# A four-byte-per-row store of zeros as the first transfer of a DMA-bound kernel

## The chip, the cores and the metric

The kernel runs on one core of a Trainium2 chip. The metric is the device time of one execution in microseconds (us). The median of three runs of the kernel before is 324.08 us, from 323.89 to 324.3.

## The reference

There are 128 samples; each is a matrix `x[b]` of 128 channels by 1024 time steps, in float32. Each sample names one of 8 subjects, and each subject has a 128 x 128 weight matrix. The sample's matrix is multiplied by its subject's weights over the channels, and the product is added to the sample:

```python
def _L0_cond_ref(x, subjects, weights):
    B, C, D, T, N_SUBJECTS = (128, 128, 128, 1024, 8)
    w = weights[subjects]
    out = jnp.einsum('bct,bcd->bdt', x, w)
    return out
x = x + _L0_cond_ref(x, itok_B_0_7, L0_cond_weights)
```

A sample is 512 KB. All of `x` is 67.1 MB read from HBM, and the output is 67.1 MB written to it; the weights of all subjects are 512 KB.

## The kernel before

The samples are taken in 32 tiles of four (`G = 2` samples in each of `H = 2` halves). The on-chip memory holds a ring of `SLOTS = 12` tiles of 2 MB, `x_all`; a tile is loaded into a slot, the products are added to it in place, and the result is stored from the same slot.

Each engine has its own list of work, written out by hand, and semaphores order the lists among one another:

- ScalarE issues all loads (the function `load`, through `transfer`, whose line in the profile is L57), one sample each, on its own transfer queue, q10. From tile 12 on it first waits until the slot's stores have landed.
- SyncE issues the load of the subject numbers (`given`, L179), the load of all weights (`w_all`, L180) and then all stores (the function `store`, L57 too), on its queue q1. A store waits for VectorE's additions (`s_added`). The first and the last tile are stored in halves, all others whole. The very last sample has a store of its own (L238), issued after ScalarE has waited for the other stores.
- VectorE clears `zeros` (L182), turns the subject numbers into indices (L192 to L198), copies the chosen weights of each sample into one of four small tiles (`place`, L152), and adds the products, which stand in PSUM, to the samples in the slot (`add`, L173).
- TensorE first multiplies zeros three times (`IDLE`, L185) and then, for each half tile, waits for the weights (`s_go`) and for the samples (`s_ready`) and does four products of 512 columns (`multiply`, L157 and L161).
- GpSimd turns the completion of loads into the semaphore `s_ready`.

Both queues run on the same 16 DMA engines. A transfer adds 16 to its semaphore when all of it has landed (`DMA = 16`). Constants such as a column of zeros (`const-float32-0.0`, 128 rows of one element) are filled by GpSimd before the lists begin.

Of the kernel before, what the change touches and what calls it, by code (L numbers as in the profile page):

```python
# [25 lines left out]
F32 = mybir.dt.float32  # L26
# [13 lines left out]
DMA = 16  # L40
# [30 lines left out]
def kernel(  # L71
# [7 lines left out]
    nc = tc.nc  # L79
    B, C, T = x.shape  # L80
# [21 lines left out]
        ctx.enter_context(nc.psum_tensor(f"ps{i}", [D, G, T], F32)).ap() for i in range(P_SLOTS)  # L102
    ]

    s_given = tc.alloc_semaphore("s_given")
    s_wall = tc.alloc_semaphore("s_wall")
    s_index = tc.alloc_semaphore("s_index")
# [11 lines left out]
    def emptied(i):  # L119
        turns = i // SLOTS  # L120
        return DMA * (H * G + 1) * turns - (DMA * G if i >= SLOTS and i % SLOTS == 0 else 0)

    def load(engine, i, q):
        transfer(
            nc,
            engine,
            xs[i % SLOTS][:, q, :],
            x[i * H * G + q].rearrange("(a r) t -> a (r t)", r=ROWS),
        ).then_inc(s_head if i * H * G + q < G else s_slot[i % SLOTS], DMA)

    def store(i, q0, q1):
        b = i * H * G
        transfer(
            nc,
            nc.sync,
            out[b + q0 : b + q1].rearrange("g d t -> d g t"),
            xs[i % SLOTS][:, q0:q1, :].rearrange("d (o g) t -> d o (g t)", g=min(G, q1 - q0)),
        ).then_inc(s_first if i == 0 and q1 == G else s_slot[i % SLOTS], DMA)

    def subjects_of(i):  # L140
        _, subject = nc.values_load_multi_w_load_instructions(
            index[0:1, i] if isinstance(i, slice) else index[0:1, bass.ds(i * (H * G), H * G)],
            engines=[mybir.EngineType.DVE],
            min_val=0,
            max_val=S - 1,
            skip_runtime_bounds_check_because="the index is clamped on the chip above",
        )
        return subject

    def place(h, subject):  # L150
        for q in range(h * G, (h + 1) * G):
            copy = nc.vector.tensor_copy(ws[q], w_all[:, bass.ds(subject[q], 1), :])  # L152
        copy.then_inc(s_go, 1)

    def multiply(slot, h):
        nc.tensor.wait_ge(s_go, 1).then_inc(s_go, -1)
        nc.tensor.wait_ge(s_ready, 1).then_inc(s_ready, -1)  # L157
        for q in range(h * G, (h + 1) * G):
            for t in range(0, T, N):
                at = slot * (H * G * T) + (q * T + t)  # L160
                mm = nc.tensor.matmul(  # L161
                    ps[h][:, q % G, t : t + N],
                    ws[q][:, 0, :],
                    x_all[:, bass.ds(at, N)],
                    start=True,
                    stop=True,
                )
        mm.then_inc(s_product, 1)

    def add(slot, h):  # L170
        mine = x_all[:, bass.ds(slot * (H * G * T) + h * G * T, G * T)]
        nc.vector.wait_ge(s_product, 1).then_inc(s_product, -1)  # L172
        nc.vector.tensor_tensor(  # L173
            mine, ps[h].rearrange("d g t -> d (g t)"), mine, ALU.add
        ).then_inc(s_added, 1)

    with tc.tile_critical():  # L177

        nc.sync.dma_start(given, subjects.rearrange("(o b) -> o b", o=1)).then_inc(s_given, DMA)  # L179
        nc.sync.dma_start(w_all, weights.rearrange("s c d -> c s d")).then_inc(s_wall, DMA)  # L180

        nc.vector.memset(zeros, 0.0).then_inc(s_zeros, 1)  # L182
        nc.tensor.wait_ge(s_zeros, 1)
        for _ in range(IDLE):
            nc.tensor.matmul(  # L185
                ps[P_SLOTS - 1][:, G - 1, :N], zeros[:, :D], zeros, start=True, stop=True
            )

        nc.vector.memset(index[:, B:], 0).then_inc(s_index, 1)  # L192
        nc.vector.wait_ge(s_given, DMA)
        nc.vector.tensor_scalar(near, given, -S, S - 1, ALU.max, ALU.min).then_inc(s_index, 1)  # L194
        nc.vector.wait_ge(s_index, 2)
        nc.vector.tensor_scalar(wrap, near, 0, S, ALU.is_lt, ALU.mult).then_inc(s_index, 1)  # L196
        nc.vector.wait_ge(s_index, 3)
        nc.vector.tensor_tensor(index[:, :B], near, wrap, ALU.add).then_inc(s_index, 1)  # L198
        for i in range(NT):
            if i == SLOTS:  # L200
                nc.scalar.wait_ge(s_first, DMA)
            if i >= SLOTS:
                nc.scalar.wait_ge(s_slot[i % SLOTS], emptied(i))
            for q in range(H * G):
                load(nc.scalar, i, q)

        for i in range(NT):
            if i == 0:
                nc.gpsimd.wait_ge(s_head, DMA * G).then_inc(s_ready, 1)
                nc.gpsimd.wait_ge(s_slot[0], DMA * G).then_inc(s_ready, 1)  # L210
            else:
                nc.gpsimd.wait_ge(s_slot[i % SLOTS], emptied(i) + DMA * H * G).then_inc(s_ready, H)

        for i in range(NT):
            for h in range(H):
                if i in (0, NT - 1) or h == H - 1:
                    nc.sync.wait_ge(s_added, i * H + h + 1)
                    store(i, h * G if i in (0, NT - 1) else 0, (h + 1) * G - (i * H + h == NT * H - 1))


        nc.vector.wait_ge(s_index, 4)
        nc.vector.wait_ge(s_wall, DMA)
        subject = subjects_of(slice(0, H * G))
        for h in range(H):
            place(h, subject)
        with nc.vector.Fori(0, NT) as turn:  # L226
            subject = subjects_of(turn + 1)
            for h in range(H):
                add(turn % SLOTS, h)
                place(h, subject)  # L230
        with nc.tensor.Fori(0, NT) as turn:
            for h in range(H):
                multiply(turn % SLOTS, h)
# [39 lines left out]
```

## Time and profile before

| What | Value |
|---|---|
| Median of three runs | 324.08 us |
| The profiled execution's own time | 324.3 us |
| Its span, first to last instruction | 322.5 us |
| Moved over HBM | 67.63 MB read, 67.11 MB written |
| Mean rate over the span | 418 GB/s |
| Mean granted TensorE clock | 0.92 |
| VectorE's additions (L173) | 64, 2291 ns each |
| Loads of a sample (512 KB) | 128, median 31.6 us from issue to landing |
| Stores of a tile (2 MB) | 30, median 47.1 us from issue to landing |
| Load of the weights (512 KB) | 5.2 us from issue to landing |

The profile is of one execution, and all its times count from the first instruction. Of each group of instructions it tells the busy time, the mean of one, and what ended the idle time before it. A view by windows gives, for chosen stretches of time, each engine's busy time with the number of its instructions, then the granted TensorE clock, the mean busy share of the 16 DMA engines, and the rate in GB/s. Bytes and busy time of a transfer packet are put down to the moment at which it starts, so that a share can exceed 1 in a short stretch. The trace also keeps a record of every single packet, with its start, length, size and queue.

### The profile page before, as it was taken

The page shows a single profiled execution, that of the slowest core. Times are in us where ns is not written, and L with a number is a line of the kernel's source. Part 1 is how long each engine was busy: PE and PEld are TensorE (multiplying, and loading weights), DVE is VectorE, ACT ScalarE, POOL GpSimd, SP SyncE. Part 2 cuts the span into 40 slices and gives each one's busy share as a digit, 9 for nine tenths or more (in the row PEclk, how much of TensorE's full clock was granted, in tenths as well). Part 3 has the DMA queues.
Part 4 walks back from the last instruction along what each step waited for, and adds up shares of the span by engine and source line. Part 5 has one row for each costly group of instructions (what it writes and reads, how often), then busy time and mean ns, then how long its engine had stood idle before and what let it go on. Part 6 is the DMA issues. An engine that isn't in the chain of part 4 may idle for free. (4 is left out here: it accounts for less than half of the span.)

```text
span 322.5 us, 2381 instructions
## 1 busy us (share of the span) xinstructions
PE 237.1 (74%) x518; PEld 98.1 (30%) x518; DVE 165.7 (51%) x202; POOL 0.2 (0%) x4
## 2 busy tenths in 40 slices
PE   5999998888888888888888888888885995500000
PEld 2434433333333333333333333333331432100000
DVE  2267776666566566666656655666666263600000
POOL 0000000000000000000000000000000000000000
PEclk9799999999999999999999999999999798955555
DMA  7999999999999999999999999999999999999996
GB/s 276 427 391 421 427 428 421 427 429 435 417 427 433 421 425 423 431 427 427 423 424 431 433 419 424 430 426 426 433 426 418 428 425 423 428 429 425 426 425 288
DMA packets 16067, 134.76 MB, mean 418 GB/s; under 512 B 2625, under 2 KB 3650, under 8 KB 3906
## 3 DMA queue, kind: packets, MB, share of 16 engines
q1 hardware_dynamic: 9922, 67.64, 50.0%
q10 hardware_dynamic: 6144, 67.12, 49.5%
q14 instruction: 1, 0.01, 0.0%
HBM read 67.63 MB, written 67.11 MB: 418 GB/s over the span
## 5 line engine op out<-in xcount | busy, mean ns | idle before, releaser
L161 PE MATMUL ps<-x_all,w 128*128 x512 | 232.7, 609 | 39.7 <-PEq L157 39.7
L173 DVE TENSOR_TENSOR x_all<-ps,x_all 128x2048 f32 x64 | 146.6, 2291 | 109.4 <-DVEq L172 109.4
L161 PEld LDWEIGHTS ps<-x_all,w 128*128 128x128 f32 x512 | 96.4, 193 | 176.0 <-issue 175.8
L152 DVE COPY w<-w_all 128x128 f32 x132 | 23.1, 218 | 4.2 <-DMA w_all<-in_L_cond_weights_dram 4.2
L185 PE MATMUL ps<-zeros 128*128 128x512 f32 x6 | 4.4, 890 | 1.7 <-DVE zeros L182 1.7
L185 PEld LDWEIGHTS ps<-zeros 128*128 128x128 f32 x6 | 1.7, 305 | 3.5 <-issue 1.9
L182 DVE MEMSET zeros<- 128x512 f32 x1 | 0.5, 485 | 1.0 <-SPq L177 1.0
L194 DVE TENSOR_SCALAR near<-given 1x128 int32<-1x128 int32 x1 | 0.2, 216 | 0.8 <-DMA given<-in_itok_B_dram 0.8
L198 DVE CUSTOM_DVE_ANT_0 index<-near,wrap 1x256 uint16<-1x256 uint16 x1 | 0.3, 278 | 0.0
L196 DVE TENSOR_SCALAR wrap<-near 1x128 int32<-1x128 int32 x1 | 0.2, 215 | 0.0
L260 POOL MEMSET const-bfloat16-1.0<- 128x1 bf16 x1 | 0.1, 101 | 0.0
L260 POOL MEMSET const-uint8-127<- 128x1 uint8 x1 | 0.1, 101 | 0.0
L260 POOL MEMSET const-float32-0.0<- 128x1 f32 x1 | 0.1, 98 | 0.2 <-issue 0.2
L260 POOL MEMSET const-float32-1.0<- 128x1 f32 x1 | 0.1, 98 | 0.0
L260 DVE BASE_LOAD x1 | 0.0, 15 | 0.1
L192 DVE MEMSET index<- 1x4 int32 x1 | 0.1, 62 | 0.0
## 6 DMA issues: line engine op xcount, KB each, us to landing
x_all<-in_x_dram ACTq DMA_DIRECT2D x128, 512.0 KB, 31.6
out_dram<-x_all SPq DMA_DIRECT2D x30, 2048.0 KB, 47.1
out_dram<-x_all SPq DMA_DIRECT2D x3, 1024.0 KB, 14.4
out_dram<-x_all SPq DMA_DIRECT2D x2, 512.0 KB, 20.6
w_all<-in_L_cond_weights_dram SPq DMA_DIRECT2D x1, 512.0 KB, 5.2
given<-in_itok_B_dram SPq DMA_DIRECT2D x1, 0.5 KB
```

Source lines behind the costliest of these rows:

```text
L152: copy = nc.vector.tensor_copy(ws[q], w_all[:, bass.ds(subject[q], 1), :])
L161: mm = nc.tensor.matmul(ps[h][:, q % G, t : t + N], ws[q][:, 0, :], x_all[:, bass.ds(at, N)], start=True, stop=True,)
L173: nc.vector.tensor_tensor(mine, ps[h].rearrange("d g t -> d (g t)"), mine, ALU.add).then_inc(s_added, 1)
L182: nc.vector.memset(zeros, 0.0).then_inc(s_zeros, 1)
L185: nc.tensor.matmul(ps[P_SLOTS - 1][:, G - 1, :N], zeros[:, :D], zeros, start=True, stop=True)
L192: nc.vector.memset(index[:, B:], 0).then_inc(s_index, 1)
L194: nc.vector.tensor_scalar(near, given, -S, S - 1, ALU.max, ALU.min).then_inc(s_index, 1)
L196: nc.vector.tensor_scalar(wrap, near, 0, S, ALU.is_lt, ALU.mult).then_inc(s_index, 1)
L198: nc.vector.tensor_tensor(index[:, :B], near, wrap, ALU.add).then_inc(s_index, 1)
L260: nc = _bacc.Bacc("TRN2", target_bir_lowering=False, num_devices=1)
```

## The change

SyncE's first transfer is now a store of zeros to the output of sample 0: the first element of each of its 128 rows, so 128 pieces of 4 bytes, 4096 bytes apart. Its source is the constant column of zeros. Behind it on the same queue come the loads of subjects and weights. Before the first real store, which writes the same addresses again, SyncE waits until the small store has landed (`s_opened`).

```diff
+    s_opened = tc.alloc_semaphore("s_opened")
     s_given = tc.alloc_semaphore("s_given")
...
     with tc.tile_critical():
 
+
+        nc.sync.dma_start(
+            out[0, :, :1],
+            nc.const_aps.tensor(0.0, (C, 1), F32),
+            allow_slow_non_contiguous=True,
+        ).then_inc(s_opened, DMA)
         nc.sync.dma_start(given, subjects.rearrange("(o b) -> o b", o=1)).then_inc(s_given, DMA)
         nc.sync.dma_start(w_all, weights.rearrange("s c d -> c s d")).then_inc(s_wall, DMA)
...
+        nc.sync.wait_ge(s_opened, DMA)
         for i in range(NT):
             for h in range(H):
                 if i in (0, NT - 1) or h == H - 1:
```

## The prediction

> **What bounds the kernel now.** I read the page first, its busy shares, slices and queues.
>
> ```profile
> span 322.5 us, 2381 instructions
> PE 237.1 (74%) x518; PEld 98.1 (30%) x518; DVE 165.7 (51%) x202; POOL 0.2 (0%) x4
> DMA  7999999999999999999999999999999999999996
> GB/s 276 427 391 421 427 428 421 427 429 435 417 427 433 421 425 423 431 427 427 423 424 431 433 419 424 430 426 426 433 426 418 428 425 423 428 429 425 426 425 288
> q1 hardware_dynamic: 9922, 67.64, 50.0%
> q10 hardware_dynamic: 6144, 67.12, 49.5%
> ```
>
> TensorE works 74% of the span and VectorE 51%. The two transfer queues (q1 is SyncE's, q10 ScalarE's) together hold the 16 DMA engines for 99.5% of it. The slices have one visible dip after the start: the third, 391 against about 426 GB/s. The windows by time locate it (the columns are busy times, the TensorE clock, the DMA share and GB/s).
>
> ```profile
> 2.00:8.00 6.00, 4.05 (x6) 1.36 (x5) 1.30 (x7) 0.00 (x0) 1.00 1.02 369
> 8.00:18.00 10.00, 9.44 (x18) 4.09 (x19) 3.15 (x5) 0.00 (x0) 0.83 1.00 424
> 18.00:24.00 6.00, 6.00 (x15) 2.46 (x13) 4.58 (x6) 0.00 (x0) 1.00 0.99 373
> 24.00:60.00 36.00, 34.01 (x78) 14.39 (x78) 24.48 (x28) 0.00 (x0) 1.00 1.01 426
> 319.00:322.50 3.50, 0.00 (x0) 0.00 (x0) 0.00 (x0) 0.00 (x0) 0.50 0.28 115
> ```
>
> From 18 to 24 us the engines are as busy as ever (0.99) and deliver 373 in place of 426 GB/s: 6 us x (1 - 373/426) = 0.75 us of transfer lost. Before it loads alone reach 424; after it loads and stores together reach 426. So neither stream is slow in itself; the change from one to the other costs something. The timeline and the waits say what starts then.
>
> ```profile
> 0.94 0.35 SPq L179 DMA_DIRECT2D given<-in_itok_B_dram  x1
> 1.35 0.42 SPq L180 DMA_DIRECT2D w_all<-in_L_cond_weights_dram  x1
> 16.40 0.65 SPq L57 DMA_DIRECT2D out_dram<-x_all  x1
> DVE w L152 <- DMA w_all<-in_L_cond_weights_dram: 4.2, 1, 4.2
> SPq L269 <- DMA out_dram<-x_all: 19.2, 1, 19.2
> ```
>
> The first store is issued at 16.40, so the dip is the first writing to HBM. The DMA view of 18 to 20.7 us sharpens it:
>
> ```profile
> q10 hardware_dynamic: 87, 0.95, 103.6%
> ```
>
> That is the only data queue listed: 4.3 us after the issue no store packet has begun. In the records of single packets the first one begins at 20.78. The weights, also issued behind queued loads, took from 1.35 to 3.80, or 2.45 us; the first store took 1.9 us more. Meanwhile load packets stretch: 16 KB takes 613 ns on average from 8 to 18 us, 979 ns from 19.5 to 20.7, with 1102 the longest, on all engines at once, and 615 from 24 to 60. Store packets take 310 ns from the first on. I read this as a price paid once, when the first writes to the output go out.
>
> **The change, part by part.** The sums are made against the profiled execution: span 322.5, and 1.8 us around it, 324.3 us. The median of the runs is 324.08, 0.22 less; I carry that to the end.
>
> The added transfer's issue on SyncE: the two neighbours took 0.35 and 0.42 us, so I take 0.4. It moves the issue of the subjects (`given`) to about 1.35 and of the weights to 1.75. VectorE waits for the weights until 7.41, then come the copies at L152, the first product at 8.56 and the first store at 16.40; all of this slips by 0.4 us, or by up to 1.9 more if the writes keep their opening delay and the weights wait behind them. The cover is ScalarE's queue: loads are issued from 0.90 until about 60 us without needing more than their slots, and 12 slots of 2 MB are 25.2 MB, 59 us at 424 GB/s. At the other end the last VectorE work ends at 281.3 us while stores run to 321, 40 us of stores in hand. So a first store 0.4 to 2.3 us late costs nothing; without that cover it would cost its whole length.
>
> The wait on `s_opened` stands on SyncE in front of the first store's wait; behind it are all stores. The transfer should land by about 6 us, and SyncE waits for VectorE until 16.40 in any case: nothing. The price comes only if the landing needs 15 us.
>
> The added packets: 128 of 4 bytes, 8 for each of 16 engines if they are spread as other 128-row transfers are. No row shows a 4-byte write to HBM. Nearest rows, from single packets: the 4-byte completion marks take 9 ns, the weights' 512-byte packets 27, the longest of these 155. That makes 0.07, 0.22 or 1.24 us per engine, all of it on the path, as the engines have no idle time. A price below nothing is excluded, since the bytes of the real store stay the same. I take 27 ns, as a data packet is nearer to it than a mark: +0.2 us. Both ends stay for the range.
>
> The opening price of 0.75 us: it should now fall at about 2 us. There all engines wait anyway, since the first load packets last up to 1167 ns in place of 613, 0.55 us more, for the first reads. If the waits for first reads and first writes lie beside each other, the 0.75 us is saved; if one follows the other it is saved at 20 us and paid at 2. Bounds: gain 0.75 to 0. I take 0.75, since the first transfers of the two queues set out within 0.04 us of each other (0.90 and 0.94), so that the two waits should begin together.
>
> Sum: 324.3 - 0.75 + 0.2 = 323.75; less 0.22 for the median, 323.5. What is late next is unchanged: the engines' bytes.
>
> **The rivals.**
>
> *The price recurs.* The dip is no first touch but what any stream of stores costs when it starts beside loads. Then eight small packets per engine open nothing: 324.08 + 0.2 = 324.3. For it speaks that the backlog of stores keeps q1 from running dry early, so the trace shows only one start. Against it: the weights started on q1 beside loads with packets at 27 ns and no stretched loads. [...]
>
> *Slower: small writes hold the engines.* The place is the head of q1, from 2 us on, ahead of subjects and weights. Each 4-byte write occupies its engine as long as the dearest 512-byte packet, 155 ns: 8 x 0.155 = 1.24 us, and the opening wait follows the first reads instead of lying beside them, so that nothing is saved: 324.08 + 1.24 = 325.3. It decides against the kernel from 81 ns per packet on if nothing is saved (0.65 us by 8), and from 175 ns if 0.75 is. For it: the write path took longest to answer of all first transfers. Against: marks of 4 bytes at 9 ns. [...]
>
> *More than the dip.* The last store's landing is set by the last of the 16 engines. After 319 us the windows hold 0.28 x 3.5 = 0.98 us of work per engine, so the mean engine ends near 319.98, and the last packet record ends at 321.13: 1.15 us of straggling. If part of that spread came from engines that opened unevenly, half of it goes too: 323.5 - 0.57 = 322.9. Against it: the completion marks of the first store are spread over 1.2 us already and had been by the second load, before any store.
>
> **How the numbers follow.** About 0.2% (0.65 us) is what a measurement of this kernel can tell from no change. The forecast, price hidden at the start: 0.56. Its own range is 323.3 (0.75 and 9 ns packets, 323.4, and a little engine spread) to 323.8 (0.45 saved with 0.2 paid), so it straddles that bound at 323.43; I give 0.30 to faster and 0.26 to the same. The price recurs: 0.12, the same. Small writes hold the engines: 0.24, slower. More than the dip: 0.08, faster. So faster 0.38, same 0.38, slower 0.24. The range goes down to the last rival's 322.9 and up to 325.2, just below the slower rival's own figure of 325.3, which leaves out its dearer half.
>
> **What would show it.** Right: with the changed kernel, the window of 18 to 24 us reads about 420 GB/s, the first store packets begin some 2.5 us after their issue, load packets there stay near 615 ns, and 2 to 8 us loses at most 0.2 us more than its 369 GB/s now. The price recurring: 18 to 24 us again near 373. Small writes: 2 to 8 us well below 369, small packets of 80 ns or more, weights landing after 9 us. Wrong altogether: DMA share below 0.98 anywhere between 24 and 319 us, which would mean that a late start is not covered.

## The result: 0.2% slower

The changed kernel takes 324.43 us (median of 19 runs, 324.01 to 324.95), the kernel before 323.88 us (19 runs, 323.38 to 324.3). The medians are 0.17% apart; the ratio worked out from all runs is 1.0020, with a 95% interval from 1.0014 to 1.0027. The forecast was 0.18% faster. The dip at the first real stores (the short loss of transfer rate when they begin) did go away, as forecast; the small store costs more than twice that at the start.

The page of the changed kernel, first its span and the slices:

```profile
span 323.0 us, 2383 instructions
DMA  6999999999999999999999999999999999999996
GB/s 216 427 425 424 424 426 427 427 426 423 426 428 428 421 433 418 428 430 417 427 432 428 419 430 420 427 430 430 417 429 430 419 435 419 425 426 428 425 427 288
```

The third slice now has 425 GB/s in place of 391, and the first has 216 in place of 276. No store runs in the third slice any more, so it alone does not show that the dip is gone; the window around the new start of the stores, further down, does. The windows of the changed kernel (busy times, TensorE clock, DMA share, GB/s) say the same with more detail:

```profile
2.00:8.00 6.00, 5.15 (x6) 1.51 (x5) 0.71 (x3) 0.00 (x0) 1.00 0.87 278
8.00:18.00 10.00, 0.00 (x0) 0.00 (x0) 0.00 (x0) 0.00 (x0) 0.65 1.03 432
18.00:24.00 6.00, 0.00 (x0) 0.00 (x0) 0.00 (x0) 0.00 (x0) 0.50 1.00 415
24.00:60.00 36.00, 28.21 (x61) 12.07 (x62) 17.54 (x23) 0.00 (x0) 0.85 1.01 427
319.00:323.00 4.00, 0.00 (x0) 0.00 (x0) 0.00 (x0) 0.00 (x0) 0.50 0.39 158
```

From 2 to 8 us the rate falls from 369 to 278 GB/s and the DMA share from 1.02 to 0.87. From 8 to 24 us TensorE and VectorE do nothing at all: their columns are zero. The timeline of SyncE, the landings (last column, us from issue) and the waits show why.

```profile
0.95 0.40 SPq L181 DMA_DIRECT2D out_dram<-const-float32-0.0  x1
1.40 0.33 SPq L186 DMA_DIRECT2D given<-in_itok_B_dram  x1
1.78 0.41 SPq L187 DMA_DIRECT2D w_all<-in_L_cond_weights_dram  x1
39.68 18.02 SPq L57 DMA_DIRECT2D out_dram<-x_all  x4
```
```profile
w_all<-in_L_cond_weights_dram SPq DMA_DIRECT2D x1, 512.0 KB, 28.3
out_dram<-const-float32-0.0 SPq DMA_DIRECT2D x1, 0.5 KB, 2.4
```
```profile
DVE w L153 <- DMA w_all<-in_L_cond_weights_dram: 23.9, 1, 23.9
DVE near L201 <- DMA given<-in_itok_B_dram: 4.6, 1, 4.6
```

The weights are issued 0.43 us later and land after 28.3 us in place of 5.2. The first real store is issued at 39.68 in place of 16.40. It costs little, as the held-back stores below show, since the loads fill the engines meanwhile (24 to 60 us: share 1.01).

In the packet records the first store packet now begins at 43.71 us. The window around it, first of the changed kernel, then of a run from the experiments whose stores are held back with no early write and begin at 48.75 us:

```profile
41.00:47.00 6.00, 6.00 (x16) 2.51 (x14) 4.79 (x6) 0.00 (x0) 1.00 1.00 422
```
```profile
46.00:52.00 6.00, 6.00 (x15) 2.42 (x14) 4.03 (x7) 0.00 (x0) 1.00 0.99 377
```

The changed kernel keeps 422 GB/s where the other falls to 377.

The packet records also show where the start is lost. The 128 small packets begin between 1.84 and 1.98 us and take 7 to 9 ns each, most of them 9. The first 16 load packets then begin at 2.97 us on average in place of 2.38 and take 1410 ns on average in place of 889. A second profile of each kernel has 2.71 in place of 2.36 us and 1567 in place of 922 ns.

For finer sums I use one more number, worked out from the records of single packets. Each packet counts as the length its size has when nothing disturbs it (16 KB 613 ns, 8 KB 309.5, 4 KB 159, 512 B 27, 4 B 9), summed and divided by 16 engines. The *lag* at a time is that time less the work moved by then. It rises where engines lose time. Packets that a version adds count as work: 128 of 4 bytes are 0.07 us per engine, 128 of 512 bytes 0.22 us, and these come on top of the lag. The *dip* is its rise from 2.5 us ahead of the first 8 KB store packet to 3 us after it. Both kernels were profiled twice:

| | lag at 10 us | dip | lag at 60 us |
|---|---|---|---|
| before | 2.68, 2.57 | 0.63, 0.61 | 3.00, 2.90 |
| changed | 3.97, 3.94 | -0.02, -0.02 | 3.52, 3.49 |

So the start loses 1.33 us, the dip saves 0.64, another 0.14 comes back in the rest of the first 60 us, and there the changed kernel is 0.55 us behind. Measured: 324.43 - 323.88 = 0.55 us. That the two agree so closely is in part luck. In the profiles, two of each kernel, the changed kernel is 0.75 us slower on average: the 16 engines end their last store 0.60 us later on average, and the last of them trails this mean by 0.19 us more.

### The profile page after: what moved, and what is told of

Read it like the earlier page. It is cut to its first block, busy times and chain, and to the rows that moved or that the text cites. A ratio compares the mean times of both kernels' runs of the same rounds, so it can differ in the third digit from the quotient of the medians.

```text
span 323.0 us, 2383 instructions
## 1 busy us (share of the span) xinstructions
PE 237.4 (73%) x518; PEld 98.6 (31%) x518; DVE 165.7 (51%) x202; POOL 0.2 (0%) x4
## 5 line engine op out<-in xcount | busy, mean ns | idle before, releaser
L192 PE MATMUL ps<-zeros 128*128 128x512 f32 x6 | 5.5, 1088 | 1.7 <-DVE zeros L189 1.7
## 6 DMA issues: line engine op xcount, KB each, us to landing
w_all<-in_L_cond_weights_dram SPq DMA_DIRECT2D x1, 512.0 KB, 28.3
```

Of the source, the lines that this page charges most:

```text
L192: nc.tensor.matmul(ps[P_SLOTS - 1][:, G - 1, :N], zeros[:, :D], zeros, start=True, stop=True)
```

## Experiments

Each time is a ratio to the kernel before, run beside it, with its 95% interval. The lag without an added transfer is that of the table, 2.62 us at 10 us on average. Edits are shown against the changed kernel, except where the text says that they start from the kernel before; lines that only declare a tile or a semaphore are left out.

### The place: behind the weights

```diff
-        nc.sync.dma_start(
-            out[0, :, :1],
-            nc.const_aps.tensor(0.0, (C, 1), F32),
-            allow_slow_non_contiguous=True,
-        ).then_inc(s_opened, DMA)
         nc.sync.dma_start(given, subjects.rearrange("(o b) -> o b", o=1)).then_inc(s_given, DMA)
         nc.sync.dma_start(w_all, weights.rearrange("s c d -> c s d")).then_inc(s_wall, DMA)
+        nc.sync.dma_start(
+            out[0, :, :1],
+            nc.const_aps.tensor(0.0, (C, 1), F32),
+            allow_slow_non_contiguous=True,
+        ).then_inc(s_opened, DMA)
```

> The small store is issued third, behind the subjects and the weights. Before loses 0.62 us between 18 and 24 us; the changed kernel has no dip there, but reaches 8 us of the profile 1.3 us further behind (lag of transferred work 4.01 against 2.70 us). Theory 'the price is that of the first writes wherever they stand': loads stall for 0.6 to 1.3 us at about 4 to 6 us, no dip when the real stores begin, 323.9 to 324.5 us beside 323.9 of before. Rival 'the place at the head is what makes it dear, since the first loads have to wait behind the writes': the stall is 0.3 us or less, and the time 323.4 to 323.6. In both the weights land within 6 us of their issue again, in place of 28.3.

Ratio 0.9999 (0.9990 to 1.0008). The lag at 10 us is 2.53, so nothing is lost. The weights land after 5.2 us. But the dip is 0.56 us, at the place where it was before, as the windows of this run show:

```profile
2.00:8.00 6.00, 4.23 (x6) 1.36 (x5) 1.28 (x7) 0.00 (x0) 1.00 1.01 369
18.00:24.00 6.00, 6.00 (x15) 2.46 (x13) 4.54 (x6) 0.00 (x0) 1.00 1.00 384
```

The same 128 writes cost 1.3 us at the head and nothing here. Some 100 of their packets move in one burst from 6.5 to 7.0 us, in which 16 load packets begin too, and those take their usual 611 ns. Both theories had assumed that the dip would go wherever the writes stand; it did not.

### One element, and two per row

```diff
-            out[0, :, :1],
-            nc.const_aps.tensor(0.0, (C, 1), F32),
+            out[0, :1, :1],
+            nc.const_aps.tensor(0.0, (1, 1), F32),
```

> The small store is one element of one row instead of 128, so that one DMA engine writes. Theory 'each engine pays for its own first write' : 15 engines keep the dip at the first real stores (about 0.6 us), one engine starts late; 323.9 to 324.3 us. Rival 'the first write opens something that all engines share': no dip, start loses 0.1 us on average; 323.3 to 323.5 us. Rival 'the 128 small writes cost by their number': start loses nothing visible, the dip is as before, 323.9 us.

Ratio 1.0006 (0.9997 to 1.0015); lag at 10 us 2.77, dip 0.41. The page counts 16069 packets in place of 16067, the piece and one completion mark, so one engine wrote; its write does not take the dip away for all.

```diff
-            out[0, :, :1],
-            nc.const_aps.tensor(0.0, (C, 1), F32),
+            out[0, :, : T // 2 + 1 : T // 2],
+            nc.const_aps.tensor(0.0, (C, 2), F32),
```

> The small store writes two elements of each row, 2 KB apart: 256 pieces of 4 bytes, 16 per engine. Theory 'the price is that of the first write, once': as the changed kernel, 324.4 to 324.6 us. Rival 'each 4-byte write costs its engine about 1.3 us / 8 = 0.16 us': 1.3 us more, 325.7 us.

Ratio 1.0030 (1.0020 to 1.0041), lag 3.42, dip 0.06. It is no clean doubling. The issue took 0.64 us and the pieces moved at 3.75 to 4.25 us, behind the first loads and not ahead of them, so the smaller loss does not refute a price per piece.

### Small reads in place of small writes

```diff
-            out[0, :, :1],
-            nc.const_aps.tensor(0.0, (C, 1), F32),
+            probe,
+            x[0, :, :1],
```

> In place of the small store SyncE first reads one element of each of 128 rows of sample 0 into a spare column; nothing is written early. Theory 'the price belongs to writes': the start is as before, the dip at the first stores stays, 323.9 to 324.1 us. Rival 'any transfer of 128 small pieces ahead of the first loads holds them up': the start loses 1.3 us, the dip of 0.6 us stays too, 325.2 us. In both the weights may land late (28 us), if it is the later issue that puts them behind the loads.

The landing of the small reads:

```profile
probe<-in_x_dram SPq DMA_DIRECT2D x1, 0.5 KB, 1.6
```

Ratio 1.0013 (1.0004 to 1.0022), lag at 10 us 2.69, dip 0.38, weights after 18.9 us. These 4-byte packets moved at the same place (1.75 to 2.25 us) and held nothing up at the start. The loss belongs to writes. The late weights do not: with reads ahead they are late too. The 0.13% is not in the lag.

### The real stores later, with no early write

```diff
+        nc.sync.wait_ge(s_slot[7], DMA * H * G)
         for i in range(NT):
             for h in range(H):
                 if i in (0, NT - 1) or h == H - 1:
```

> The kernel before, with one wait added: SyncE issues the first store only when tile 7 has been loaded (about 42 us), no early write. Over the runs so far the dip at the first real stores is 0.62 us where they begin at 21 us (before), 0.56 at 21 (small writes behind the weights), 0.4 at 34 to 35, 0.07 and 0 at 43 (small writes first). Theory 'the dip depends on how late the stores begin, not on an earlier write': dip 0.1 us or less, 323.2 to 323.5 us, 0.1 to 0.2% faster than before. Rival 'an early write at the head takes the dip away': dip 0.6 us near 43 us, the time as before, 323.8.

SyncE's first store in this run:

```profile
44.52 21.95 SPq L57 DMA_DIRECT2D out_dram<-x_all  x7
```

Ratio 0.9995 (0.9986 to 1.0004), dip 0.54 us. Holding back the first store by 28 us costs nothing that can be measured, so the cover named in the prediction is real; and a late start alone does not take the dip away.

### Fewer, wider and narrower pieces

Sixteen rows at the head:

```diff
-            out[0, :, :1],
-            nc.const_aps.tensor(0.0, (C, 1), F32),
+            out[0, ::8, :1],
+            nc.const_aps.tensor(0.0, (C // 8, 1), F32),
```

> The small store at the head writes 16 rows instead of 128, one element of each eighth row, so one piece per engine if they are spread. Theory 'the loads behind the writes wait for as many write answers as each engine has pieces': the start loses 0.2 us, not 1.3, and the time is 323.5 to 323.9. Rival 'the first write's answer is waited for once, whatever the number': 1.3 us lost at the start, 324.4.

Ratio 1.0013 (1.0004 to 1.0022); lag 2.91, dip 0.52. The page counts 16099 packets in place of 16067, the 16 pieces and 16 completion marks, which I take as one piece per engine. With that the loss is 0.3 us, not 1.3; an eighth of 1.33 would be 0.17, so the loss is not shown to be proportional to the pieces.

Then 512 bytes of each row, and 4 bytes from the same tile behind the same wait:

```diff
+        nc.vector.memset(blank, 0.0).then_inc(s_blank, 1)
+        nc.sync.wait_ge(s_blank, 1)
         nc.sync.dma_start(
-            out[0, :, :1],
-            nc.const_aps.tensor(0.0, (C, 1), F32),
+            out[0, :, :128],
+            blank[:, :128],
```

> The store at the head writes 512 bytes of each of 128 rows instead of 4, from a tile that VectorE clears first; SyncE waits for that, so the issue is some 0.4 us later than in the changed kernel. Beside it runs the next kernel with 4 bytes at the same place. [...] Rival 'any write ahead of the first loads is dear': 1 us or more at the start, 324.3 to 324.8.

> As the run of 512-byte pieces, but 4 bytes of each row, from the same cleared tile and behind the same wait. [...] If it loses nothing, the 0.4 us of later issue, behind the first loads, is what matters.

Ratios 1.0017 (1.0008 to 1.0026) and 1.0024 (1.0015 to 1.0033). At 10 us the lag is 2.85 with 512 bytes and 3.30 with 4: the narrow pieces lose 0.45 us more although they carry 128 times less. The dips are 0.45 and 0.31 us. Both moved among the first loads (the narrow ones from 3.80 to 4.11 us, where they lose 0.68 us against before), which is why the pair was repeated at the head, below.

### The weights later, second profiles, and half the rows

The kernel before, with the weights issued later:

```diff
+        nc.sync.wait_ge(s_zeros, 1)
         nc.sync.dma_start(w_all, weights.rearrange("s c d -> c s d")).then_inc(s_wall, DMA)
```

> The kernel before, with the issue of the weights held back until VectorE has cleared the zeros (1.6 us in place of 1.35), and no early write. In every run with a small transfer ahead the weights were issued 0.3 to 0.8 us later and landed after 18 to 28 us in place of 5; those runs came out 0.1 to 1 us above before, the two runs with early weights did not. Theory 'a late landing of the weights costs time by itself': weights land after 15 us or more, 0.3 to 0.4 us above before, 324.1. Rival 'late weights are covered by the queue of loads': the weights land as late, the time is that of before, 323.8. If the weights land early again, it is the small transfer ahead and not the later issue that puts them behind.

Ratio 1.0007 (0.9998 to 1.0016), weights issued at 1.63 us and landing after 15.9, lag 2.69, dip 0.61. An issue 0.28 us later is enough to make them late. What it costs is within the interval: anything from nothing to 0.5 us.

The kernel before and the changed kernel, unedited, once more each:

> The kernel before once more, for a second profile. Expected if the profile shown is typical: loads start without an extra wait (lag of transferred work 2.7 us at 10 us), the dip at the first stores is 0.6 us, and the last of the 16 DMA engines ends 0.5 to 1.1 us behind their mean.

> The changed kernel once more, for a second profile. Theory 'the small writes hold up the first loads in every execution': lag 3.5 to 4 us at 10 us. Theory 'and they take the dip away': no dip near 43 us. Rival 'the missing dip was this one execution's': a dip of 0.3 to 0.6 us, as in all runs but two.

These are the second profiles in the table above (ratios 0.9998 and 1.0024). The loss at the start and the missing dip are in both profiles taken of the changed kernel.

Every second row at the head:

```diff
-            out[0, :, :1],
-            nc.const_aps.tensor(0.0, (C, 1), F32),
+            out[0, ::2, :1],
+            nc.const_aps.tensor(0.0, (C // 2, 1), F32),
```

> The small store at the head writes 64 rows, every second one, so 4 pieces per engine if they are spread. At 10 us of the profile the lag was 2.7 us with none, 2.9 with one per engine, 4.0 with eight. Theory 'the loss at the start grows with the pieces per engine, 0.16 us each': lag 3.3 us, 324.2 us. Rival 'it is all or nothing': lag 2.9 or 4.0.

Ratio 1.0035 (1.0022 to 1.0047), lag 3.08, dip 0.31. Inconclusive for the count: the pieces moved at 3.75 to 4.25 us.

### Width at the head

Here the two kernels with the cleared tile get the same wait in front of the loads, so that the writes stand ahead of them:

```diff
+        nc.scalar.wait_ge(s_blank, 1)
         for i in range(NT):
             if i == SLOTS:
                 nc.scalar.wait_ge(s_first, DMA)
```

> 512-byte pieces at the head, 8 per engine, with the first loads held back by the same wait as the store (0.3 us), so that the writes stand ahead of the loads as in the changed kernel. Theory 'the 4 bytes are what is dear': start loses the 0.3 us of the wait and 0.2 more, lag 3.1 to 3.3 us at 10 us. Rival 'writes that stand ahead of the first loads are dear, whatever their size': lag 4.2 us.

> As the run of 512-byte pieces at the head, with 4 bytes. Both theories: the changed kernel's loss and the wait of 0.3 us, lag 4.2 to 4.3 us at 10 us, no dip when the stores begin, 324.7 us.

The window of 2 to 12 us, first of the 512-byte run, then of the 4-byte run:

```profile
2.00:12.00 10.00, 5.28 (x6) 1.64 (x6) 0.71 (x3) 0.00 (x0) 0.96 0.99 367
```
```profile
2.00:12.00 10.00, 5.29 (x6) 1.65 (x6) 0.71 (x3) 0.00 (x0) 0.97 0.87 329
```

The lag at 10 us is 3.15 and 4.40: with place, count, address and source tile alike, 4 bytes in place of 512 cost 1.25 us more. Of the wide run's 0.52 us over before, 0.44 is the later first load packet (2.68 us in place of 2.23), so wide writes ahead of the loads lose about 0.1 us, and their own packets take 0.22 us where the narrow ones take 0.07. With that the narrow pieces are 1.1 us dearer. Part of it is the first load packet: it begins at 3.38 us with narrow pieces. The dip of the wide run is 0.14, that of the narrow one -0.02. The ratios are 1.0025 (1.0015 to 1.0035) and 1.0031 (1.0020 to 1.0042): the start of the narrow run is far worse, and its time hardly. The two profiled executions are 0.57 us apart, the medians only 0.06; the lag at 60 us is 2.97 and 3.92. Where the rest of the wide run's time goes is taken up under the end of the last engine below, and is not settled.

### Half the rows at the head, and another sample

```diff
-            out[0, :, :1],
-            nc.const_aps.tensor(0.0, (C, 1), F32),
+            out[0, : C // 2, :1],
+            nc.const_aps.tensor(0.0, (C // 2, 1), F32),
```

> As the changed kernel with the first 64 rows, so 4 pieces per engine. The run with every second row did not answer its question: its issue took 0.56 us in place of 0.40, and its pieces moved at 3.75 to 4.25 us, among the first loads. Theory 'the loss at the head grows with the pieces per engine': from 0.25 us (one) and 1.3 (eight) follows a lag of about 3.3 us at 10 us if the pieces again move by 2.1 us. Rival 'all or nothing': 2.9 or 4.0.

Ratio 1.0040 (1.0026 to 1.0054), lag 3.53, dip 0.11. Again the issue took 0.56 us and the pieces moved late, so the count stays known from one and eight per engine only.

```diff
-            out[0, :, :1],
+            out[B - 1, :, :1],
```

> As the changed kernel, but the zeros go to the last sample of the output, 66.6 MB away from where the first real store writes. Two profiles of the changed kernel agree: 1.3 us lost at the start (lag 3.94 to 3.97 at 10 us against 2.57 to 2.68), no dip near 43 us. Theory 'the early writes leave the engines or the write path in a state': the same loss and no dip, 324.4 us. Rival 'they prepare the addresses that the first store uses': the same loss at the start, and the dip of 0.6 us is back, 325.0 us.

> Zeros to the last sample of the output at the head, a second profile. The first showed lag 3.13 us at 10 us and a dip of 0.36, where the changed kernel twice showed 3.94 to 3.97 and none. If the address matters: 3.1 to 3.2 and a dip of 0.3 to 0.6 again. If that run was an odd one: 3.9 and no dip.

Ratios 1.0022 (1.0013 to 1.0031) and 1.0023 (1.0013 to 1.0034). The windows of the first of the two:

```profile
2.00:12.00 10.00, 5.14 (x6) 1.50 (x5) 0.71 (x3) 0.00 (x0) 0.96 1.00 374
12.00:60.00 48.00, 33.12 (x70) 13.98 (x71) 20.79 (x27) 0.00 (x0) 0.80 1.01 422
```

Lag 3.13 and 3.14, dip 0.36 and 0.16. Neither theory had this: 4-byte writes at the same moment lose 0.5 us in the last sample and 1.3 us in the first, and they take away a part of the dip only. The address matters for both.

### Wide pieces behind the weights

The small store at the head is taken out and a wide one put behind the weights:

```diff
         nc.sync.dma_start(w_all, weights.rearrange("s c d -> c s d")).then_inc(s_wall, DMA)
+        nc.sync.wait_ge(s_zeros, 1)
+        nc.sync.dma_start(out[0, :, :D], zeros[:, :D]).then_inc(s_opened, DMA)
```

> Pieces of 512 bytes of zeros to the first sample, issued behind the weights. At the head 4-byte pieces lose 1.3 us at the start, 512-byte ones 0.1 beside the wait; behind the weights 4-byte pieces lose nothing but leave a dip of 0.56 us. Theory 'a write that costs nothing also prepares nothing': no loss at the start, dip 0.5 to 0.6 us, 323.8 us. Rival 'enough bytes written early take the dip away, wherever they stand': dip 0.2 us or less, 323.3 us, faster than both kernels.

Ratio 1.0007 (0.9997 to 1.0016), lag 2.57, dip 0.61. Here, too, writes that lose nothing at the start leave the dip. No version was clear of the kernel before on the faster side.

## Why the prediction was wrong, point by point

**The term that failed is the added packets, +0.2 us at 27 ns each.** Their records do show 9 ns, less than I took. But the record of a 4-byte write is not its price: the loads behind it begin later (2.97 us in place of 2.38) and take longer (1410 ns in place of 889). The start loses 1.33 us beside the 0.07 us of the records, so the term measures 1.4 us in place of 0.2. The step that failed is to price the added packets by the length of a packet record and to put nothing on what waits behind them. With the two measured terms, 1.4 and 0.64, the prediction's sum comes to 324.8 us, on the side that was measured; 0.2 us of what it has over 324.43 is that the kernel before ran at 323.88 in its 19 runs. Runs place the loss: reads of 4 bytes at the same place lose nothing (lag 2.69 us), 512-byte writes 0.1 us beside the later first load and their own 0.22 us, 4-byte writes behind the weights nothing (lag 2.53), and 4-byte writes among the first loads 0.68. The full loss takes writes, narrow ones, standing ahead of the first loads.

The prediction has small writes as its slower rival, with 1.24 us. Its size is near by luck: it let each 4-byte packet occupy its engine for 155 ns, and the records show 9. Its signs came true for the rate from 2 to 8 us (278 GB/s) and the late weights (28.3 us), not for packets of 80 ns or more. It was also wrong in letting nothing be saved, since the dip went.

With place, count and address alike, the two runs at the head put the loss at about 0.1 us for 512 bytes and about 1.35 us for 4. Why narrow writes are the dearer ones is not shown: no record tells what an engine does inside, and behind the weights the lag shows no cost of the same writes (2.53 us at 10 us, against 2.62 without them).

**The dip of 0.75 us saved: right in sign and nearly in size.** By the windows of 18 to 24 us I had 0.75; by the lag it is 0.62, and it is gone in both profiles of the changed kernel. So not every start of stores beside loads pays it. But the rival that the price recurs is right about the two runs with early writes behind the weights, where it was paid in full (0.56 and 0.61).

**The late first store packet was misread.** The prediction counted the 1.9 us by which the first store came later than the weights among the signs of an opening price, and expected 2.5 us from issue to first packet once it was paid. In the changed kernel 4.03 us pass (39.68 to 43.71), in place of 4.38 before: the delay returned, and yet there is no dip. So the late packet is not part of the dip's price.

**That the price is hidden at about 2 us** holds at most for wide pieces at the head, with 0.1 us of lag beside the later first load, 0.22 us of packets of their own, and a dip of 0.14.

**A write opens the path once: not so simple.** The dip is 0.54 us with stores held back, 0.61 with late weights, 0.56 and 0.61 with early writes behind the weights. It is fully absent (-0.02) only where 4-byte pieces to the first sample stand ahead of the loads, eight per engine, and nearly so with sixteen per engine among the first loads (0.06). With small reads it is 0.38, with no write to open anything. Over all twenty profiles the dip is smaller the more the start has lost: 0.38 to 0.63 us where the lag at 10 us is at most 2.91, 0.06 to 0.36 where it is 3.08 to 3.53, none from 3.94 on. No run changed the lag alone, so this is a pattern and not a cause. Why the dip goes stays open: a first touch of addresses does not explain the writes behind the weights, a state of the engines does not explain the last sample.

**The cover of the late start: right, and far more was asked of it.** I allowed 0.4 to 2.3 us; the first store came 23 us later. The run that held it back 28 us was not slower (ratio 0.9995).

**The end of the last engine**, my fourth case, moves the time by itself, and against what that case hoped for. The trail is the time by which the last of the 16 completion marks of the last store follows their mean. It is 1.07 and 0.40 us in the two profiles of before (324.3 and 323.49 us), 1.04 and 0.80 in those of the changed kernel, and 2.11 with the first 64 rows. Of the twelve profiles in which several small or wide pieces were written ahead of the loads or among the first, eleven have a trail of 0.80 us or more and one 0.50; of the other eight, seven have 0.72 or less and one 1.07. So the early writes seem to lengthen it. That is how kernels with a lag like before's at 60 us still came out slower. With every second row the lag there is 3.01, and all six runs (324.43 to 325.27 us) lie above all runs of the kernel before beside them (up to 324.3); its trail is 1.48. With the wide pieces at the head (2.97) the trail is 1.00, and their own packets add 0.22 us. What spreads the engines was not tested.

## What to carry to other kernels

In a kernel whose DMA engines have no idle time, price a tiny transfer by what waits behind it, not by its bytes or its record: here 128 writes of 4 bytes cost 1.3 us ahead of the first loads, 0.7 among them and nothing at 6.5 us, behind the weights. A stall that disappears where you aimed is no gain until the place it moved to has been read in the same profile. And compare several profiles of the same kernel before explaining half a microsecond: two executions of the kernel before differ by 0.8 us, 0.7 of it in how far the last engine trails the mean.

## What was not expected of the hardware

In these runs the landing of the weights depends sharply on the moment of issue. Issued at 1.35 to 1.37 us, behind one transfer, they land after 5.0 to 5.2 us; at 1.63 us after 15.9; at 1.66 to 2.31 us and behind a further transfer after 18 to 29. In the packet records the early ones move in a burst from 3.8 to 6.2 us. With the issue at 1.63 us the burst is there too, half of the packets having begun by 4.8 us, but the last tenth begins from 8.2 to 17.0 us. In the changed kernel half of them begin after 12.2 us, in turns with the loads: from 12 to 20 us 295 packets of 512 bytes and 198 load packets of 16 KB.

The same 4-byte writes at the same moment lose 1.3 us at the start when they go to the first sample and 0.5 when they go to the last, in two profiles each.
